# A two-layer block with gathered attention: the last group of tokens cut in two halves

## The chip, the cores and the metric

The kernel runs on one core of a Trainium2 chip. Its time is device time in microseconds (us), from the start of the program to its end; the median of 17 runs is 2808.39 us (2798.34 to 2819.59). A measurement of this kernel can tell about 0.2% from no change.

## The reference, cut to what matters

The input x holds 2048 tokens of 128 channels, float32. Two layers are applied, each an attention and a set of experts, each on a layernorm of x and added to x:

```
x = x + attention0(layernorm(x))   # 16 heads of 64, dense softmax over all 2048 tokens
x = x + experts0(layernorm(x))     # 16 gated experts, the best 4 of the best 2 of 4 groups, weighted
x = x + attention1(layernorm(x))   # 96 chosen tokens for each query, then softmax over these
x = x + experts1(layernorm(x))     # one shared gated expert and 2 of 8 experts by the token's number
```

For attention1 an indexer gives a score to every earlier token:

```
s_i = relu(einsum('bthd,bsd->bths', q_i, k_i));  I = einsum('bths,h->bts', s_i, idx_w)
I = where(local, inf, I); I = where(causal, -inf, I)      # the last 64 tokens are always chosen
_, idx = top_k(I, 96)
key, value = (c_kv @ W_uk)[idx], (c_kv @ W_uv)[idx]       # gathered for each query
```

So attention1 of a token needs experts0's result for that token and for all the tokens before it, since their keys may be chosen. experts0 and experts1 work on each token by itself.

## The kernel before

The 2048 tokens are 16 tiles of 128 tokens, and four tiles make a group: g = 0 to 3, tiles 4g to 4g+3. Attention 0 is a stream of units in `run` and takes most of the span. What follows it for a group is `follow(g)` (L588): `experts0`, `attention1`, `experts1`, in that order, each a generator whose yields carry a cost in us. For groups 0 to 2 it is advanced in small steps between the steps of attention 0 of the next group. For group 3 nothing is left beside it: `self.alone` is set, its PSUM tiles (`self.x`, L138) come from all eight banks in turn, and the generator is run through to its end. This stretch, from 2456 us on, is what the change touches; tiles 12 to 15 are its tokens.

What an engine does next is set by the order in which the program issues the work, with a scheduler that may move instructions on the engines' queues (not those marked to be kept in program order). SBUF pools are stacks on two sides, left and right; a new pool waits for the memory of what stood there before.

**First experts** (`experts0`, L599). For four tiles: the weights wb are loaded by SyncE (SP), six experts ahead; layernorm; four transposes on PE and a copy (`transposed`, L145); then `hidden` (L710) for the first four experts: the products p1 and p3 over 512 columns (L714, L715), Tanh and Identity on ACT (thb, zb; L718, L719), two instructions on DVE (hb; L721, L722). Then the gate: products pg, a sigmoid out of Exp, and the ranks by comparing all pairs (`below`), many small instructions on DVE; its weights are transposed on PE. Then expert after expert: `hidden` of expert e+4, the four products py of expert e-1 (one for each tile of 128 tokens) and four additions on DVE into the residual xr, which stays in SBUF.

**Second attention** (`attention1`, L727). It starts with a load of the ACT function set that holds Exp and Ln together. Preparation, for four tiles at once: layernorm, transposes, keys pk, softplus (L87 to L89: Exp, Ln on ACT, mu on DVE), a store of the keys kg into a table in HBM (SP), four products pm for the indexer's keys and queries, rotation of the keys and their transposes. Then, tile after tile:

- `index_scores(n)` (L792): the scores against all earlier tokens, in blocks of 512 columns by four heads: a product pi (L802), Relu on ACT into one of six buffers rl (L807), and an accumulation on DVE (L804, L808).
- `choose(n)` (L824): four rounds over all columns on DVE (the eight largest, their indices, and their removal: 11 passes), a transpose of the indices (ixT, L842), and then 32 indirect DMAs issued by POOL (`gather`, L853) that fetch the chosen tokens' keys from the table, 128 rows each.
- `queries(n)` (L866): loads of the local window by SP, the product pq, softplus on ACT, rotation on DVE, transposes ptq on PE into qT (three buffers).
- `attend(n)` (L913): rotation of the gathered keys kv, transposes ptr, products pl against the local window and the chosen keys (L956), maximum on DVE (mx, L962), Exp on ACT (L966), transposes, the products po, pj and at last xr += pj (L1013).

In the last group the order is written out: scores and choice of tiles 12 and 13; scores of 14 beside the queries of 12 and its choice beside the attention of 12; the same for 15 beside 13; then queries and attention of 14, then of 15.

**Last experts** (`experts1`, L1055), for four tiles at once: the ten weights wd are loaded, layernorm, transposes and a copy xT (L1069); two shared hidden layers (p1d, p3d); 16 small products ph for the eight experts, Gelu on ACT; the products pyd (L1097, L1102), yT (L1107), transposes pty (L1114), the sum o (L1116), and the store of the output.

Of the kernel before, what the change touches and what calls it, by code (L numbers as in the profile page):

```python
# [8 lines left out]
F32 = mybir.dt.float32  # L9
# [3 lines left out]
ALU = mybir.AluOpType  # L13
# [93 lines left out]
class Program:  # L107
# [37 lines left out]
    def transposed(self, src, dst, name):  # L145

        pt = self.x(name)
        for j in range(4):
            self.nc.tensor.transpose(pt[:, j, :], src[:, j, :], self.ident)
        self.nc.scalar.copy(dst, pt.rearrange("p a b -> p (a b)"))  # L150
# [437 lines left out]
    def follow(self, g):  # L588

        for stage in (self.experts0, self.attention1, self.experts1):  # L590
            with ExitStack() as sc:
                yield from stage(sc, g)
# [6 lines left out]
    def experts0(self, sc, g):  # L599
        nc, w, xr = self.nc, self.w, self.xr[g]  # L600
        sm = sc.enter_context(self.tc.tile_pool(name="b_sm", bufs=1, side="right"))

        ahead = 4 if self.alone else 0
        hp = sc.enter_context(self.tc.tile_pool(name="b_h", bufs=2 + ahead, side="right"))
        wp = sc.enter_context(self.tc.tile_pool(name="b_w", bufs=4 + ahead, side="right"))
        wx = [self.weights(wp, e, f"wb{g}_{e}") for e in range(2 + ahead)]
        xn = sm.tile([P, 4, C], F32, tag="xn", name=f"xn1_{g}")
        layernorm(nc, sm, xr, xn, "ln1")
        yield 5.0
        xT = sm.tile([P, 512], F32, tag="xT", name=f"xT1_{g}")  # L610
# [14 lines left out]
        pg = self.x(f"pg{g}", [P, 4, NE0])  # L625
        for j in range(4):
            nc.tensor.matmul(pg[:, j, :], xT[:, j * P : j * P + P], w["wg"], start=True, stop=True)
        s = sm.tile([P, 4, NE0], F32, tag="s", name=f"gs{g}")
# [8 lines left out]
        def below(v, n, first, k, tag):  # L637

            shape = [P, 4, n, n]
# [4 lines left out]
            ff = bcast(first.rearrange("p a b -> p (a b)"), 1, 4)  # L644
# [3 lines left out]
            rank = sm.tile([P, 4, n], F32, tag="rank" + tag, name=f"rank{tag}{g}")  # L648
# [4 lines left out]
        gm = sm.tile([P, 4, NG0], F32, tag="gm", name=f"gm{g}")  # L653
# [4 lines left out]
        goff = sm.tile([P, 4, NG0], F32, tag="goff", name=f"goff{g}")  # L658
        nc.vector.tensor_scalar(goff, gsel, 1.0, None, ALU.subtract)
        ms = sm.tile([P, 4, NE0], F32, tag="ms", name=f"ms{g}")  # L660
# [7 lines left out]
        we = sm.tile([P, 4, 32], F32, tag="we", name=f"we{g}")  # L668
        wh = sm.tile([P, 4, NE0], F32, tag="wh", name=f"wh{g}")
        nc.vector.memset(we, 0.0)  # L670
        nc.vector.tensor_tensor(we[:, :, 0:NE0], s, esel, ALU.mult)
        ws = sm.tile([P, 4], F32, tag="ws", name=f"ws{g}")
        wr = sm.tile([P, 4], F32, tag="wr", name=f"wr{g}")
# [6 lines left out]

        pt = self.x(f"ptw{g}", [P, P])
        nc.tensor.transpose(pt, we.rearrange("p a b -> p (a b)"), self.ident)
        wt = sm.tile([P, P], F32, tag="wt", name=f"wt{g}")
        nc.scalar.copy(wt, pt)
        yield 1.0
        pb = self.x(f"pb2_{g}")
        nc.tensor.matmul(pb.rearrange("p a b -> p (a b)"), wt, w["b2"], start=True, stop=True)
# [4 lines left out]
        for e in range(NE0 + 1):  # L692
# [5 lines left out]
            if e > 0:  # L698
                h = hs.pop(e - 1)
                py = self.x(f"py{g}_{e}")  # L700
                for j in range(4):
                    nc.tensor.matmul(py[:, j, :], h[:, j * P : j * P + P], wx[e - 1][:, 2, :], start=True, stop=True)
                yield 1.0
                for j in range(4):
# [5 lines left out]
    def hidden(self, pool, wx, xT, b1, hb1, b3, name):  # L710

        nc = self.nc
        p1, p3 = self.x("p1" + name, [P, 512]), self.x("p3" + name, [P, 512])
        nc.tensor.matmul(p1, wx[:, 0, :], xT, start=True, stop=True)  # L714
        nc.tensor.matmul(p3, wx[:, 1, :], xT, start=True, stop=True)  # L715
        th = pool.tile([P, 512], F32, tag="th", name="th" + name)
        z = pool.tile([P, 512], F32, tag="z", name="z" + name)
        nc.scalar.activation(th, p1, AF.Tanh, scale=0.5, bias=hb1)  # L718
        nc.scalar.activation(z, p1, AF.Identity, bias=b1)  # L719
        h = pool.tile([P, 512], F32, tag="h", name="h" + name)  # L720
# [4 lines left out]
    def attention1(self, sc, g):  # L725
# [7 lines left out]
        cols = slice(512 * g, 512 * g + 512)  # L733
# [4 lines left out]
        with ExitStack() as prep:  # L738
            pp = prep.enter_context(tc.tile_pool(name="c_prep", bufs=1, side="right"))
            xn = pp.tile([P, 4, C], F32, tag="xn", name=f"xn2_{g}")  # L740
            layernorm(nc, pp, xr, xn, "ln2")
            yield 5.0
            xT = pp.tile([P, 512], F32, tag="xT", name=f"xT2_{g}")
            self.transposed(xn, xT, f"pt2_{g}")
# [3 lines left out]
            pk = self.x(f"pk{g}", [P, 4, 64])  # L748
            for j in range(4):
                nc.tensor.matmul(pk[:, j, :], xT[:, j * P : j * P + P], w["wck"], start=True, stop=True)  # L750
            kg = pp.tile([P, 4, 64], F32, tag="kg", name=f"kg{g}")
# [494 lines left out]
```

## Time and profile before

| | |
|---|---|
| median of 17 runs | 2808.39 us (2798.34 to 2819.59) |
| the profiled execution | 2808.99 us |
| its span, first to last instruction | 2807.2 us |
| mean granted TensorE clock over the span | 0.938 |
| busy in the span: PE / DVE / ACT / POOL | 2543.4 (91%) / 1671.4 (60%) / 1789.5 (64%) / 674.1 us (24%) |
| the same up to 2456 us | 2320.0 / 1429.8 / 1659.7 / 544.0 us |
| the same from 2456 us on, 351.2 us | 223.5 / 241.6 / 129.8 / 130.1 us |

The busy shares of the whole span tell of attention 0, where PE works 94% of the time. In the last 351.2 us no engine is busy all the time: PE 64%, DVE 69%. A line of a timeline gives the start in us, the length in us, the engine, the line of the program, the operation, out<-in with the shapes, and in brackets the idle time of the engine before it and what ended it. "issue" there means that the engine waited for nothing that the profile shows. A line of the table of windows gives a stretch, its length, each engine's busy time with the number of its instructions, the granted TensorE clock, and what the DMA engines did.

### The profile page before, as it was taken

Reading aid. Unit: us, or ns where it says so; the run is one execution under the profiler, and the core shown is the slowest. Engines: PE = TensorE matmul, PEld = TensorE weight load, DVE = VectorE, ACT = ScalarE, POOL = GpSimd, SP = SyncE. Lnnn points to the kernel's source line nnn. Section 1 sums busy time; section 2 is a strip of 40 time slices with the busy share of each in tenths; the row PEclk is TensorE's granted clock in tenths of the full one; section 3 lists DMA queues with packets and bytes.
Section 4 is the critical chain, followed back from the end, with each engine's and each line's share of the span. In section 5 each row is a group of like instructions: output and inputs, shape, how many; then the busy total and the mean of one; then the engine's idle time right before and its main releaser. Section 6 shows DMA issues by size and latency. Waiting matters only on the chain. (4 is left out here: it accounts for less than half of the span.)

```text
span 2807.2 us, 39304 instructions
## 1 busy us (share of the span) xinstructions
PE 2543.4 (91%) x13452; PEld 1175.0 (42%) x13452; DVE 1671.4 (60%) x4650; ACT 1789.5 (64%) x4192; POOL 674.1 (24%) x964
## 2 busy tenths in 40 slices
PE   6999999999979999999999999999989999976566
PEld 3444444434434444434334444444433444442344
DVE  7655554566664454566686455466587754278863
ACT  3777778766656776856666677765656677533344
POOL 2111110000166620000065630000055460001771
PEclk9999999999999999999999999999999999986567
DMA  4322221111112211111111211111111120100111
GB/s 133 90 61 58 57 60 46 44 47 46 30 40 47 50 38 55 44 40 46 34 41 42 47 41 52 42 50 46 27 38 37 38 50 16 63 23 11 25 26 39
DMA packets 98103, 127.79 MB, mean 46 GB/s; under 512 B 31344, under 2 KB 49776, under 8 KB 97904
## 3 DMA queue, kind: packets, MB, share of 16 engines
q1 hardware_dynamic: 81520, 108.48, 13.8%
q0 software_dynamic: 16384, 16.81, 3.1%
q8 instruction: 106, 1.74, 0.3%
q14 instruction: 93, 0.76, 0.1%
HBM read 115.26 MB, written 9.96 MB: 45 GB/s over the span
## 5 line engine op out<-in xcount | busy, mean ns | idle before, releaser
L340 ACT ACTIVATE neg<-neg,mx 128x512 f32<-128x512 f32 x1024 | 729.8, 714 | 311.1 <-DVE neg L329 302.7
L329 DVE TENSOR_SCALAR_CACHE_REDUCE neg<-pa 128x512 f32<-128x512 f32 x1024 | 657.9, 685 | 430.1 <-PE pa L323 425.2
L390 ACT ACTIVATE e<-pb 128x512 f32<-128x512 f32 x1024 | 550.4, 595 | 296.5 <-PE pb L386 280.9
L384 PE MATMUL pb<-q,kb 64*128 64x512 f32 x2048 | 643.2, 631 | 7.4 <-DVE t_q L302 4.1
L323 PE MATMUL pa<-ka,q 64*128 64x512 f32 x2048 | 601.6, 623 | 19.3 <-ACT e L390 13.5
L853 POOL DMA_INDIRECT kv<-table,ixT x512 | 507.0, 990 | 425.7 <-DVE v L804 268.5
L399 PE MATMUL po<-e,ckv 128*64 128x512 f32 x2048 | 508.3, 610 | 0.0
L323 PEld LDWEIGHTS pa<-ka,q 64*128 64x128 f32 x2048 | 247.3, 191 | 225.7 <-issue 102.2
L303 POOL TENSOR_TENSOR q<-t_q 128x512 f32<-128x512 f32 x32 | 40.7, 1273 | 1200.8 <-DVE t_q L302 1099.8
L384 PEld LDWEIGHTS pb<-q,kb 64*128 64x128 f32 x2048 | 226.9, 190 | 209.0 <-issue 108.2
L386 PE MATMUL pb<-mrow,onesb 64*128 64x512 bf16 x1024 | 254.0, 385 | 8.1 <-ACT mrow L375 8.1
L399 PEld LDWEIGHTS po<-e,ckv 128*64 128x64 f32 x2048 | 126.7, 137 | 299.8 <-issue 282.3
L340 ACT ACTIVATION_READ_ACCUMULATOR neg<-neg,mx 128x1 f32 x1024 | 192.6, 188 | 0.0
L802 PE MATMUL pi<-kiT,qiT 64*128 64x512 f32 (+4 forms) x320 | 115.9, 624 | 24.8 <-DVE v L804 14.4
L850 POOL COPY at<-kv 128x1 f32<-128x1 f32 x378 | 80.0, 216 | 183.4 <-DMA kv<-table,ixT 176.8
L386 PEld LDWEIGHTS <-onesb 64*128 64x128 bf16 x1024 | 69.4, 96 | 128.6 <-issue 120.5
L418 DVE SCALAR_TENSOR_TENSOR xr<-pp,rs,xr 128x128 f32<-128x128 f32 x256 | 72.2, 344 | 84.5 <-PE pp L415 72.3
L721 DVE SCALAR_TENSOR_TENSOR hb<-thb,zb 128x512 f32<-128x512 f32 x64 | 44.3, 692 | 114.1 <-ACT zb L719 114.1
L808 DVE SCALAR_TENSOR_TENSOR v<-rl,iw_sb,v 128x512 f32<-128x512 f32 (+4 forms) x120 | 76.4, 642 | 50.7 <-ACT rl L807 46.6
L303 POOL TENSOR_TENSOR kst<-t_k 128x512 f32<-128x512 f32 x32 | 41.0, 1281 | 264.4 <-DVE t_k L302 168.5
L966 ACT ACTIVATE e<-pl,mx 128x208 f32<-128x208 f32 x128 | 54.3, 429 | 78.0 <-DVE mx L963 74.0
L962 DVE TENSOR_REDUCE mx<-pl 128x2 f32<-128x416 f32 x64 | 37.6, 590 | 97.2 <-PE pl L956 96.8
(276 smaller groups left out, 2862.9 us busy)
## 6 DMA issues: line engine op xcount, KB each, us to landing
ka<-kd SPq DMA_DIRECT2D x128, 256.0 KB
kb<-kd SPq DMA_DIRECT2D x128, 256.0 KB
wb<-in_wx SPq DMA_DIRECT2D x64, 192.0 KB
kd<-kst SPq DMA_DIRECT2D x32, 256.0 KB
kv<-table,ixT POOLq DMA_INDIRECT x512, 2.5
wd<-in_wx SPq DMA_DIRECT2D x40, 192.0 KB
csk<-in_cs SPq DMA_DIRECT2D x4, 512.0 KB
csq<-in_cs SPq DMA_DIRECT2D x4, 512.0 KB
```

Of the source, the lines that this page charges most:

```text
L303: nc.gpsimd.tensor_tensor(dst, t[:, 0, :], t[:, 1, :], ALU.add)
L323: nc.tensor.matmul(ps[h], q[rows, qt * P : qt * P + P], k[rows, :], start=True, stop=True)
L329: nc.vector.tensor_scalar(t, ps[h], -1.0, None, ALU.mult, ALU.min, accum_out=mx[at])
L340: nc.scalar.activation(t, t, AF.Exp, bias=mx[at], scale=-1.0, accum_out=su[at])
L384: nc.tensor.matmul(ps[h], k[rows, c], q[rows, :], start=True, stop=False)
L386: nc.tensor.matmul(ps[h], self.onesb[rows, :], mrow[rows, :], start=False, stop=True)
L390: nc.scalar.activation(e[:, h, :], ps[h], AF.Exp)
L399: nc.tensor.matmul(self.pos[u][cols, :], self.ckv[:, kb, :], e[:, h, :], start=(kb == 0), stop=(kb == NT - 1))
L802: nc.tensor.matmul(pi[:, : hi - lo], qiT[h // 2][rows, q], kiT[rows, lo:hi], start=True, stop=True)
L808: nc.vector.scalar_tensor_tensor(v[:, lo:hi], rl[:, : hi - lo], w["iw"][:, h : h + 1], v[:, lo:hi], ALU.mult, ALU.add)
L850: tc.keep_in_program_order(nc.gpsimd.tensor_copy(at[:, i : i + 1], slot))
L853: nc.gpsimd.indirect_dma_start(out=kv[:, 2 * (g % 16) + g // 16, :], out_offset=None, in_=table[0 : P * (n + 1), :], in_offset=bass.Indire ...
```

## The change

Only the last group is touched (`self.alone`); the functions take the first tile t0 and the number of tiles nt, and groups 0 to 2 call them with 0 and 4 as before.

- The first experts run for tiles 12 and 13, then the preparation for these two. The first experts of tiles 14 and 15 and their preparation (`rest`) are issued in between the scores and choices of tiles 12 and 13, two yields of `rest` for one of these. Products and ACT and DVE instructions that were 512 columns wide are 256 wide; the weights wb are loaded twice.
- The scores, choices, queries and attentions of 14 and 15 beside 12 and 13 keep their order.
- After the choice of 15: the weights wd are loaded; queries and attention of 14, queries of 15, then the last experts of tiles 12 and 13, the attention of 15, and the last experts of tiles 14 and 15. Each has its own store of the output.
- Alone, the pools of first and last experts stand on the left side; rl has four buffers instead of six, qT two instead of three.

In the built programs PE has 6323 instructions instead of 6227 (matrix products and transposes with their sequencer's rows), DVE 3247 instead of 3100, ACT 2968 instead of 2904, SP 472 instead of 454, POOL as many as before.

```
     def follow(self, g):
-        for stage in (self.experts0, self.attention1, self.experts1):
+        with ExitStack() as sc:
+            yield from self.experts0(sc, g, 0, 2 if self.alone else 4)
+        with ExitStack() as sc:
+            yield from self.attention1(sc, g)
+        if not self.alone:
             with ExitStack() as sc:
-                yield from stage(sc, g)
+                yield from self.experts1(sc, g, 0, 4, self.last_weights(sc, g))
...
-    def experts0(self, sc, g):
-        nc, w, xr = self.nc, self.w, self.xr[g]
+    def experts0(self, sc, g, t0, nt):
+        nc, w, xr = self.nc, self.w, self.xr[g][:, t0 : t0 + nt, :]
+        side, g = "left" if self.alone else "right", f"{g}_{t0}"
...
-                for j in range(4):
+                for j in range(nt):
                     nc.vector.scalar_tensor_tensor(
                         xr[:, j, :], py[:, j, :], wh[:, j, e - 1 : e], xr[:, j, :], ALU.mult, ALU.add
                     )
...
-        p1, p3 = self.x("p1" + name, [P, 512]), self.x("p3" + name, [P, 512])
+        n = xT.shape[1]
+        p1, p3 = self.x("p1" + name, [P, n]), self.x("p3" + name, [P, n])
...
-        with ExitStack() as prep:
+        def prepare(prep, t0, nt):
+            cols = slice(512 * g + P * t0, 512 * g + P * (t0 + nt))
+            part = slice(P * t0, P * (t0 + nt))
...
+        with ExitStack() as prep:
+            yield from prepare(prep, 0, 2 if self.alone else 4)
...
-                        rl = sm.tile([P, 512], F32, tag="rl", name=f"rl{n}_{lo}_{h}", bufs=6 if self.alone else 2)
+                        rl = sm.tile([P, 512], F32, tag="rl", name=f"rl{n}_{lo}_{h}", bufs=4 if self.alone else 2)
...
-                t = sm.tile([P, P, NH1], F32, tag=f"qT{i}", name=f"qT{n}_{i}", bufs=3 if self.alone else 1)
+                t = sm.tile([P, P, NH1], F32, tag=f"qT{i}", name=f"qT{n}_{i}", bufs=2 if self.alone else 1)
...
         if self.alone:
-            for m in range(n, n + 4):
-                if m < n + 2:
-                    yield from index_scores(m)
-                    yield from choose(m)
-                else:
-                    yield from beside(1, index_scores(m), queries(m - 2))
-                    yield from beside(3, choose(m), attend(m - 2))
-            for m in range(n + 2, n + 4):
-                yield from queries(m)
-                yield from attend(m)
+            def rest():
+                with ExitStack() as sb:
+                    yield from self.experts0(sb, g, 2, 2)
+                with ExitStack() as prep:
+                    yield from prepare(prep, 2, 2)
+
+            first = itertools.chain(*(f(m) for m in (n, n + 1) for f in (index_scores, choose)))
+            yield from beside(2, first, rest())
+            for m in (n + 2, n + 3):
+                yield from beside(1, index_scores(m), queries(m - 2))
+                yield from beside(3, choose(m), attend(m - 2))
+
+            with ExitStack() as sd:
+                wx = self.last_weights(sd, g)
+                yield from queries(n + 2)
+                yield from attend(n + 2)
+                yield from queries(n + 3)
+                with ExitStack() as sf:
+                    yield from self.experts1(sf, g, 0, 2, wx)
+                yield from attend(n + 3)
+                yield from self.experts1(sd, g, 2, 2, wx)
             return
...
-    def experts1(self, sc, g):
-        nc, w, xr = self.nc, self.w, self.xr[g]
-        sm = sc.enter_context(self.tc.tile_pool(name="d_sm", bufs=1, side="right"))
-        wp = sc.enter_context(self.tc.tile_pool(name="d_w", bufs=10, side="right"))
-        wx = [self.weights(wp, NE0 + i, f"wd{g}_{i}") for i in range(10)]
-        xn = sm.tile([P, 4, C], F32, tag="xn", name=f"xn3_{g}")
+    def experts1(self, sc, g, t0, nt, wx):
+        nc, w, xr = self.nc, self.w, self.xr[g][:, t0 : t0 + nt, :]
+        at, g, nj = 4 * g + t0, f"{g}_{t0}", 16 * nt
+        sm = sc.enter_context(self.tc.tile_pool(name="d_sm", bufs=1, side="left" if self.alone else "right"))
+        xn = sm.tile([P, nt, C], F32, tag="xn", name=f"xn3_{g}")
...
+    def last_weights(self, sc, g):
+        pool = sc.enter_context(self.tc.tile_pool(name="d_w", bufs=10, side="left" if self.alone else "right"))
+        return [self.weights(pool, NE0 + i, f"wd{g}_{i}") for i in range(10)]
```

## The prediction

> **What bounds the kernel now.** I read first the table of windows over the last 350 us of the span, cut at the borders of the last group's stages; then the timelines of POOL and DVE across those borders; then the chain that ended last. The two built programs show that nothing ahead of this stretch moves but a few short DVE instructions, so all of the answer lies here.
>
> ```profile
> core 0: us, PE busy (x) PEld busy (x) DVE busy (x) ACT busy (x) POOL busy (x), PEclk, DMA share, GB/s
> 2456.00:2527.00 71.00, 50.92 (x219) 31.05 (x216) 56.23 (x159) 22.52 (x36) 0.00 (x0) 0.83 0.08 23
> 2527.00:2543.00 16.00, 10.92 (x30) 5.47 (x32) 6.09 (x33) 4.66 (x10) 0.00 (x0) 0.58 0.05 9
> 2543.00:2582.00 39.00, 25.71 (x78) 9.43 (x74) 37.90 (x50) 14.88 (x32) 0.00 (x0) 0.68 0.06 8
> 2582.00:2711.00 129.00, 72.88 (x494) 42.54 (x494) 109.21 (x147) 43.69 (x107) 98.56 (x96) 0.57 0.14 25
> 2711.00:2753.00 42.00, 27.31 (x262) 21.83 (x262) 15.20 (x41) 23.62 (x61) 31.55 (x32) 0.70 0.14 26
> 2753.00:2777.00 24.00, 18.64 (x213) 14.33 (x212) 5.92 (x16) 13.04 (x37) 0.00 (x0) 0.71 0.01 3
> 2777.00:2807.00 30.00, 17.09 (x84) 11.51 (x84) 11.03 (x36) 7.37 (x9) 0.00 (x0) 0.73 0.23 75
> ```
>
> The rows are: first experts; preparation; scores and choice of tile 12; choices of 13 to 15 beside the gathers; the last gathers beside attention 14; attention 15; last experts. DVE is full in the third row and 85% busy in the fourth. The POOL and DVE timelines at their edges:
>
> ```profile
> 2582.76 1.52 POOL L853 DMA_INDIRECT kv<-table,ixT  x1 [257.00 <-DVE v L804]
> ...
> 2709.32 0.94 POOL L853 DMA_INDIRECT kv<-table,ixT  x1 [0.30 <-issue]
> 2711.97 0.94 POOL L853 DMA_INDIRECT kv<-table,ixT  x1 [1.71 <-issue]
> ...
> 2751.53 1.45 POOL L853 DMA_INDIRECT kv<-table,ixT  x1 [0.30 <-issue]
> ```
>
> ```profile
> 2711.02 0.21 DVE L842 STREAM_TRANSPOSE ixT<-ix 128x32 uint32<-128x32 uint32 x1
> 2716.10 0.29 DVE L1013 TENSOR_TENSOR xr<-xr,pj 128x128 f32<-128x128 f32 x1 [4.87 <-PE pj L1012]
> ...
> 2745.21 0.29 DVE L1013 TENSOR_TENSOR xr<-xr,pj 128x128 f32<-128x128 f32 x1 [10.80 <-PE pj L1012]
> ```
>
> Once started, the 128 gathers run almost without a gap, 42.2 us for 32; the one gap, 1.71 us, waits for tile 15's choice (call the end of the choice of tile n Tn: T12 2581.8, T13 2611.2, T14 2658.4, T15 2711.2). So POOL and DVE are balanced: DVE's list ends just when POOL runs dry. After T15 there is a second balance: attention 14 and the queries of 15 end on PE at 2753.1, the last gather at 2753.0. Only then come attention 15 (to 2776.9) and the last experts (to 2803.9, plus 3.3 for the output).
>
> **First experts by two tiles.** PE takes 2.61 us an expert in the steady part (p1 0.86, p3 0.86, py 0.89), DVE 2.31 (0.61+0.65 for hb, 4x0.26 for xr). DVE instructions shrink less than by half: 0.69 us at 128x512 (L721), 0.42 at 128x256 (mu, L89), so 0.34 and 0.38 start to start; two tiles cost 1.24 on DVE, 1.31 on PE. Gating: five 128x1024 instructions of 1.25 fall to about 0.7 (-2.7), small ones stay. Layernorm and transposes save 1.4, the first four experts about 4. The stage ends at 2500.6 instead of 2526.6: -26 (bounds -20, if ACT and semaphores hold an expert to 1.7 us, and -30). The weights now lie in memory that the big attention frees, behind its last loads on SP: issue 2453 to 2455 instead of 2404. At 0.49 us an issue and 0.6 us a load (192 KB at 323 GB/s in the last experts' loading) the first is there by 2458, needed at 2463.5; xn's layernorm covers it, without it up to 5 us.
>
> **Preparation by two tiles.** 16.5 us from the last xr to the first score becomes 11.8: the fixed chain of 14 tiny instructions (0.2 each) stays, four products at the half clock go from 1.7 to 0.86 each. The first score stands at 2512.4, 30.7 early.
>
> **Scores and choice of 12, now with the second half of the first experts between.** DVE order, counted: 11 passes over 1600 columns 19.6; scores 8.7; gating 7.5; 15 hidden layers 10.4; 18 additions to xr 4.7; rest 0.7: 51.6 us busy where before there were 37.9. Idle I add 8: Tanh's table load and the first four experts 5.5, the transposed gate weights 2.1 (3.3 in the row before). T12 = 2512.4 + 59.6 = 2572.0: 30.7 early has become 9.8.
>
> **T13.** 37.1 busy (choice 21.1, scores 9.2, the last 14 additions 3.6, layernorm and hidden rest) + 1.5 idle: 2610.6, level with before.
>
> **T14.** Before, 47.3 us, 5.4 of it a wait for gathers. Now tile 14's keys are prepared only here: 1.4 us of layernorm, then transposes, pk, four products, first score: 8.1 us, while DVE has nothing else in its order. Then 42.9 busy (scores 10.4, choice 22.8, queries and attention of 12 the rest) and 10 idle (6.0 as in tile 13's attention, where PE's pl is awaited; 2.5 for table loads, below; 1.5 at the first score): 61.0, T14 = 2671.6, 13.2 late. POOL has then been dry since 2657.
>
> **T15.** The same block as before (52.8) with one exposed table load: 54.1, T15 = 2725.7, **14.5 late**. As a check, DVE work from 2456.4 to T15 grows from 209 to 219 us, idle from 45 to 50.
>
> **Table loads.** The built order has 15 loads in this stretch instead of 3, because Tanh evicts the set that held both Exp and Ln; then Ln and Exp swap for every tile.
>
> ```profile
> 2783.34 1.02 ACT L1069 COPY xT<-pt 128x512 f32<-128x512 f32 x1 [10.28 <-issue]
> 2784.38 1.28 ACT L718 ACT_TABLE_LOAD   x1
> 2786.53 0.69 ACT L718 ACTIVATE thd<-p1d,hb 128x512 f32<-128x512 f32 x1 [0.87 <-PE p1d L714]
> ```
>
> A load takes 1.28 and waits for nothing, so it hides where ACT idles; Exp's loads ahead of the softmax do (ACT waits 2.0 there for tile 14), Ln's follow Exp directly and do not: 2.5 for tile 12 (two loads), 1.3 each for 13, 14, 15. [...] The rows show 1.28 (the instruction after 2419.27+1.28 starts at 2420.56).
>
> **After T15.** Before, 96.3: 5.1 to xr 13; 29.1 to xr 14; 7.9 queries 15; 23.9 attention 15; 27.0 layernorm and experts; 3.3 out. Now 5.1; 31.2 (one load, layernorm instructions between); 9.2 (one load); then the last experts of tiles 12 and 13, in PE's order between ptq and the transposes of kv 15, so wholly on the path; attention 15 at the pace of 14 (22.9); layernorm 4.1; experts again; out 3.2. One experts pass: 21.8 from its transposes to o, less 3.0 (p1, p3 by half), 0.9 (hb, Gelu), about 2.7 (copies, pyd, yT, pty, o); the 64 small products stay, 32 of them take 3.5 at 0.11 each whatever they stream: 15.0 and, second time, 14.7 (bounds 11.5 and 21.8, since no row has these at 32 columns). Sum 105.4: **9 longer**. The 42 us of tile 15's gathers would cover 42 us of work, but 60 stand there, and T14 to T15 leaves POOL so early that the gathers end at 2770, long before attention 15 at 2785.
>
> **Sum.** 2725.7 + 105.4 = 2831.1 of span, +23.9 on 2807.2. The profiled execution took 2808.99, 1.8 around its span and 0.6 above the median: 2832.
>
> **The other edits.** The fewer buffers (rl 6 to 4, qT 3 to 2) I cost at nothing: DVE, not ACT, paces the scores; if rl stalls, 0.5 us a block of four, 6 at most. SP: table<-kg of tiles 14 and 15 stands behind ten wd loads (4.9 us), but these wait only for the second experts, 10 us before kg; window loads follow it. The last output is half as large.
>
> **Rivals.** (a) The front's gain survives: PE and ACT fill DVE's waits better, first experts -30, the gap at 8.1 halved, T15 at 2714; end near 2820. For it: DVE idles 45 us before. Chance 0.19. (b) The interleaving stalls: 8 PSUM banks shared by p1, p3, py and pi, PE in order and at clock 0.5 as in the gathers' row; 1 us for each of 12 experts: 2844. Chance 0.15. (c) **Faster**: the gathers stay the bound. They begin at 2572.9 and need 168.8; the end is 2741.7 + 1.5 + 23.9 + 4.1 + 14.7 + 3.2 = 2789.1, 2791 with what lies around it. It decides if T15 falls by 2699 and the last experts fit beside the gathers; DVE's busy sum alone, 219 us from 2456.4, puts T15 at 2675 with no idle at all. Chance 0.10. (d) The halves cancel: T15 comes 9 us early and pays for the tail, 2809. Chance 0.07. That the order is not changed as said is excluded by the built order.
>
> **How the numbers follow.** Forecast 2832 (2824 to 2840), chance 0.49. The range 2815 to 2848 takes in (a) and most of (b); it leaves out (c), (d) and the upper part of (b), some 0.2. Faster by over 0.2% (5.6 us, about what a measurement of this kernel can tell from no change) is (c), 0.10; within it (d), 0.07; slower 0.83.
>
> **What would show it.** Right: ixT's four transposes at about 2572, 2611, 2672, 2726; POOL idle some 14 us ahead of tiles 14 and 15 each; 15 table loads; pyd of tiles 12 and 13 ahead of ptr of 15, and attention 15 starting well after its gathers. Wrong: gathers without a gap, or attention 15 waiting for kv.

## The result, and the profile after

The changed kernel takes 2867.14 us (median of 8 runs, 2861.54 to 2871.05) against 2807.4 us for the kernel before (46 runs): a ratio of 1.0209, 95% interval 1.0194 to 1.0223. It is slower by 59.7 us, where 24 were forecast and 2848 was the top of the range. The profiled execution has a span of 2865.7 us, 58.5 more than before.

The last addition of attention 0 into xr (xr<-pp) is the same event in all kernels; it moves by a few us from execution to execution, so all stages below are counted from it. Tn is again the end of tile n's choice, read here at the start of the transpose ixT, 0.2 us ahead of the forecast's reading; xr and o are read at the start of their additions.

| stage, us | before | forecast | after |
|---|---|---|---|
| attention 0 to T12 | 123.1 | 113.5 | 113.4 |
| to T13 | 29.3 | 38.6 | 43.8 |
| to T14 | 47.3 | 61.0 | 68.7 |
| to T15 | 52.8 | 54.1 | 56.9 |
| to xr of 13 | 5.1 | 5.1 | 5.1 |
| to xr of 14 | 29.1 | 31.2 | 32.7 |
| to o of tiles 12 and 13 | - | 24.2 | 30.5 |
| to xr of 15 | 31.7 | 22.9 | 27.2 |
| to the last o | 26.3 | 18.8 | 27.5 |
| to the end of the span | 4.0 | 3.2 | 3.7 |
| sum | 348.7 | 372.6 | 409.4 |

T12 and the first experts (to 2499.8, forecast 2500.6) came as worked out. From T12 to T15 the time is 15.7 longer than forecast, behind T15 21.2. The table of windows of the changed kernel, cut at these events (columns as before: busy us of PE, its weight loads, DVE, ACT, POOL, then the granted clock):

```profile
2500.00:2512.00 12.00, 7.68 (x22) 4.36 (x22) 6.30 (x50) 3.14 (x11) 0.00 (x0) 0.57 0.36 117
2512.00:2570.00 58.00, 42.02 (x153) 25.90 (x152) 51.63 (x110) 20.97 (x49) 0.00 (x0) 0.76 0.12 30
2570.00:2613.50 43.50, 17.93 (x48) 8.31 (x44) 37.53 (x68) 5.23 (x11) 31.28 (x32) 0.58 0.26 70
2613.50:2682.30 68.80, 46.25 (x271) 25.36 (x272) 46.80 (x77) 32.10 (x74) 31.22 (x32) 0.60 0.11 20
2682.30:2739.30 57.00, 36.59 (x257) 20.93 (x256) 45.03 (x65) 25.17 (x58) 32.96 (x32) 0.64 0.10 19
2739.30:2777.00 37.70, 25.93 (x245) 21.14 (x246) 13.70 (x47) 21.20 (x52) 28.14 (x30) 0.64 0.14 25
...
2786.00:2808.00 22.00, 18.24 (x94) 16.11 (x93) 3.79 (x9) 7.60 (x13) 0.00 (x0) 0.66 0.00 0
2808.00:2834.80 26.80, 20.99 (x211) 15.48 (x210) 7.20 (x20) 13.84 (x37) 0.00 (x0) 0.56 0.03 7
2834.80:2865.70 30.90, 20.72 (x80) 18.25 (x80) 7.22 (x27) 4.38 (x8) 0.00 (x0) 0.50 0.02 5
```

DVE's busy time to T15 is 220 us, as forecast (219). Its idle time is 63 us, 13 more than allowed: 6 in the third row (choice of 13), 22 in the fourth, 12 in the fifth. In the last three rows the granted clock falls from stage to stage and ends at 0.50 flat; 80 instructions of PE take 20.7 us there, 84 that stream twice the columns took 17.1 before. POOL, which had one gap of 1.71 us before, now waits twice:

```profile
2682.62 0.94 POOL L866 DMA_INDIRECT kv<-table,ixT  x1 [28.02 <-DVE ixT L855]
2740.02 0.94 POOL L866 DMA_INDIRECT kv<-table,ixT  x1 [14.99 <-issue]
...
2779.50 0.94 POOL L866 DMA_INDIRECT kv<-table,ixT  x1 [0.30 <-issue]
```

The gathers end at 2780.4, and attention 15 begins at 2807. So the gathers had long ceased to bind, as forecast.

### The profile page after: what moved, and what is told of

Read it like the earlier page. It is cut to its first block, busy times and chain, and to the rows that moved or that the text cites. A ratio compares the mean times of both kernels' runs of the same rounds, so it can differ in the third digit from the quotient of the medians.

```text
span 2865.7 us, 39838 instructions
## 1 busy us (share of the span) xinstructions
PE 2593.9 (91%) x13603; PEld 1221.5 (43%) x13603; DVE 1686.8 (59%) x4769; ACT 1814.3 (63%) x4256; POOL 670.3 (23%) x964
## 3 DMA queue, kind: packets, MB, share of 16 engines
q1 hardware_dynamic: 83856, 111.63, 13.9%
## 4 chain that ended last, share of the span: by engine, by line
PE 61%; DVE 14%; DMA 8%; ACT 7%; issue 4%; POOL 3%; SPq 0%; DVEq 0%; ACTq 0%; POOLq 0%
PE pb L385 13%; PE pa L324 12%; PE po L400 11%; DMA kv<-table,ixT 7%; DVE neg L330 3%; ACT neg L341 3%; POOL kv L866 3%; PE pb L387 3%; PE py L711 2%; PE p1b L724 2%; PE pp L416 2%; PE p3b L725 2%; PE pl L963 1%; PE pl L969 1%; DVE ix L850 1%
## 5 line engine op out<-in xcount | busy, mean ns | idle before, releaser
L866 POOL DMA_INDIRECT kv<-table,ixT x512 | 500.8, 978 | 460.0 <-DVE v L817 258.9
L400 PEld LDWEIGHTS po<-e,ckv 128*64 128x64 f32 x2048 | 126.8, 137 | 301.2 <-issue 284.7
L815 PE MATMUL pi<-kiT,qiT 64*128 64x512 f32 (+4 forms) x320 | 119.0, 624 | 16.2 <-DVE v L817 6.0
L731 DVE SCALAR_TENSOR_TENSOR hb<-thb,zb 128x512 f32<-128x512 f32 (+1 forms) x80 | 46.6, 583 | 113.7 <-ACT zb L729 113.6
L975 DVE TENSOR_REDUCE mx<-pl 128x2 f32<-128x416 f32 x64 | 37.7, 590 | 102.1 <-PE pl L969 101.7
```

What stands on the lines that cost most here:

```text
L400: nc.tensor.matmul(self.pos[u][cols, :], self.ckv[:, kb, :], e[:, h, :], start=(kb == 0), stop=(kb == NT - 1))
L815: nc.tensor.matmul(pi[:, : hi - lo], qiT[h // 2][rows, q], kiT[rows, lo:hi], start=True, stop=True)
L866: nc.gpsimd.indirect_dma_start(out=kv[:, 2 * (g % 16) + g // 16, :], out_offset=None, in_=table[0 : P * (n + 1), :], in_offset=bass.Indire ...
```

## The experiments

The front is what lies before T15, the end what lies behind it. Profiled stages in us, each from one profiled execution, and the ratio of the runs to the kernel before on the same chip. Where an edit leaves the front alone it still moved by up to 2.4 us (250.7 instead of 252.5, 280.4 instead of 282.8), so a difference of some 2 us in one profile says little.

| kernel | front | end | ratio (95% interval) |
|---|---|---|---|
| before | 252.5 | 96.2 | 1 |
| changed | 282.8 | 126.6 | 1.0209 (1.0194 to 1.0223) |
| last experts by four | 282.5 | 101.7 | 1.0127 (1.0095 to 1.0160) |
| first experts by four | 250.6 | 121.2 | 1.0074 (1.0053 to 1.0094) |
| keys of 14, 15 early | 266.6 | 126.8 | 1.0187 (1.0148 to 1.0226) |
| small products of 64 columns | 280.6 | 117.3 | 1.0170 (1.0133 to 1.0206) |
| one table load | 282.5 | 116.4 | 1.0171 (1.0138 to 1.0203) |
| rotation of 15 first | 280.4 | 123.3 | 1.0192 (1.0162 to 1.0222) |
| last experts beside attention 14 | 282.9 | 115.3 | 1.0170 (1.0134 to 1.0206) |
| early keys, one load, last by four | 272.2 | 102.0 | 1.0091 (1.0059 to 1.0123) |
| before, PE filled (18) | 250.7 | 93.0 | 1.0001 (0.9988 to 1.0015) |

Five more runs stand in two disturbed batches (told below), against the kernel before in the same batch: 64 columns with PE filled 1.0134 (1.0093 to 1.0174) and again 1.0181 (1.0134 to 1.0229), the first experts in two halves 1.0144 (1.0098 to 1.0189) and again 1.0126 (1.0072 to 1.0179), the kernel before with 12 filling products 1.0022 (0.9995 to 1.0049).

**Undoing one half of the change.** In the first kernel the last experts run once, for four tiles:

```
-    with ExitStack() as sf:
-        yield from self.experts1(sf, g, 0, 2, wx)
     yield from attend(n + 3)
-    yield from self.experts1(sd, g, 2, 2, wx)
+    yield from self.experts1(sd, g, 0, 4, wx)
```

> The changed kernel with its last experts again for four tiles at once, after attention 15; first experts by halves as changed. The profiled span after (2865.7 us) splits at the end of tile 15's choice: 2739.3 before it (2711.0 in the kernel before) and 126.4 behind it (96.3 before). Theory 1, the two halves of the loss are independent: the choice of 15 still ends near 2739, the rest takes the 96.3 of before plus up to 4 for ACT table loads, span 2836 to 2840, about 30 slower than before. Rival, the long end comes from elsewhere (colder PE, table loads, attention 14 and 15 themselves): the rest takes 110 or more, span above 2849.

In the second the first experts and the preparation do:

```
-    yield from self.experts0(sc, g, 0, 2 if self.alone else 4)
+    yield from self.experts0(sc, g, 0, 4)
...
-    yield from prepare(prep, 0, 2 if self.alone else 4)
+    yield from prepare(prep, 0, 4)
...
-    yield from beside(2, first, rest())
+    for m in (n, n + 1):
+        yield from index_scores(m)
+        yield from choose(m)
```

> The changed kernel with first experts and preparation again for four tiles at once, ahead of all scores; the last experts by halves as changed. Theory 1: the choice of 15 ends as in the kernel before, at 2711 to 2714 (fewer rl buffers may cost up to 3), and the end takes 120 to 126 (no exchange of ACT tables between Ln and Exp, up to 6 less than after): span 2831 to 2840. Rival, the long end is caused by the late front (a colder PE, gathers out of step): the end takes 105 or less, span below 2819.

Theory 1 holds, though both spans (2840.3 and 2830.2) lie just outside their ranges: 35.5 us remain with the split of the first experts alone, 23.0 with that of the last alone, together 58.5 of the 60.7. Within that the two losses add up. The second kernel keeps the fewer buffers of rl and qT, and its choices of 14 and 15 take 46.4 and 53.2 us (47.3 and 52.8 before): these buffers cost nothing that shows, as forecast. From xr of 15 to the last o, the last experts take 27.5 us for two tiles and 26.3 for four: halving them saved nothing, so one of the two passes is pure addition. (24.4 in two other kernels, told under the clock.)

**The clock.** 32 of the small products ph in the kernel before, and in the changed kernel PE in the small products of the first pass, then in the last pass:

```profile
2790.46 3.68 PE L1087 MATMUL ph<-xT,wd 128*128 128x64 f32 x32
```

```profile
2790.95 3.74 PE L1110 MATMUL ph<-xT,wd 128*128 128x32 f32 x32
...
2799.00 6.87 PE L1125 MATMUL pyd<-ge,wd 128*128 128x32 f32 x32
...
2842.84 1.06 PE L725 MATMUL p3d<-xT,wd 128*128 128x256 f32 x2
2843.70 6.88 PE L1110 MATMUL ph<-xT,wd 128*128 128x32 f32 x32
2850.38 1.20 PE L1120 MATMUL pyd<-hd,wd 128*128 128x256 f32 x2
2852.69 1.22 PE L1120 MATMUL pyd<-hd,wd 128*128 128x256 f32 x2 [1.11 <-DVE hd L732]
2853.70 6.87 PE L1125 MATMUL pyd<-ge,wd 128*128 128x32 f32 x32
```

In the first pass ph starts at the full clock and takes 0.11 us an instruction, as with 64 columns in the kernel before; but the granted clock falls to 0.50 at 2794.4, behind 3.4 us of these products, and pyd takes 0.21. In the last pass PE is never idle from 2840.1 to 2851.6, and yet the granted clock stays at 0.50: 0.21 us each. In the experiment each small product, and the two pyd products of the shared layers, stream their columns twice; the weights that they load, and what is kept of the result, stay the same:

```
-    ph = self.x(f"ph{g}_{k}", [P, 8, nj])
+    ph = self.x(f"ph{g}_{k}", [P, 8, wide, nj])
...
-    nc.tensor.matmul(ph[:, r, :], wx[2 + CHOSEN[r][k]][:, 0, :], xT[:, r, :], start=True, stop=True)
+    nc.tensor.matmul(ph[:, r, :, :], wx[2 + CHOSEN[r][k]][:, 0, :], bcast(xT[:, r, :], 1, wide), start=True, stop=True)
...
```

> The changed kernel, with every small product of its last experts (and their two pyd products of the shared layers) streaming its columns twice, so 64 instead of 32 columns (512 instead of 256), results as before. Theory 2: the granted clock stays or falls to 0.5 in the last experts because a product of 32 columns keeps PE occupied by its weights, not by its stream; with 64 columns 96 of the 128 small products that took 0.21 each take 0.11 again, span 2856 to 2860 (6 to 10 us shorter than after). Rival, only the pauses of PE between stages set the clock: nothing gets warmer, the wider products cost up to 3 us, span 2866 to 2869.

The timeline of PE there, in the last pass:

```profile
2834.80 1.06 PE L725 MATMUL p3d<-xT,wd 128*128 128x256 f32 x2
2835.65 4.46 PE L1111 MATMUL ph<-xT,wd 128*128 128x64 f32 x32
2839.95 1.08 PE L1125 MATMUL pyd<-hd,wd 128*128 128x512 f32 x2
...
2843.10 3.68 PE L1128 MATMUL pyd<-ge,wd 128*128 128x64 f32 x32
```

Twice the columns of ph in two thirds of the time (4.46 us instead of 6.88), and those of pyd in 3.68 instead of 6.87, which is what 32 products of 64 columns take at a granted 1.00 in the kernel before. From 2826.7 on the mean granted clock is 0.70, where it was 0.50. The pass takes 21.8 us instead of 27.5, and the end 117.3 instead of 126.6 (9.3 less, 6 to 10 expected). Part of the 5.7 in the pass can be chance: in two kernels with 32 columns (one table load, and last experts beside attention 14) the last pass took 24.4. The two ge, which wait for ph on DVE, start 2.10 and 1.95 us apart there instead of 3.41, and the mean granted clock of that stretch is 0.56 in the first of the two. But for pyd DVE waits 7.98 us there, as in the last pass of every profiled kernel with 32 columns; with 64 columns it waits 4.74. The pauses of PE in the pass are the same with 32 and 64 columns (4.31 and 4.32, 0.68, 1.11 and 0.71 us), and so are the weights loaded: in these runs the number of columns streamed makes the difference. The next one also fills PE's idle time ahead of the last experts and in the queries and attention of 15 with bf16 products whose results are overwritten:

```
+    for _ in range(k if self.alone else 0):
+        self.tc.keep_in_program_order(self.nc.tensor.matmul(out[:, 0:n], self.identb, rows, start=True, stop=True))
```

> The changed kernel with small products of 64 columns as in the run on them, and idle time of PE at the end filled by products whose result is overwritten: 18 (256 columns, bf16) ahead of the transposes of each of the two last experts, 10 and 8 (416 columns) ahead of the transposes ptq and pte of tile 15. Stretches are compared by what lies between xr of tile 14, o of the first half, xr of tile 15, o of the second half: 30.5, 27.2 and 27.5 us in the changed kernel, 28.2, 26.0 and 21.8 with 64 columns alone. Theory 2, the granted clock is what these stretches lack: o to xr 23 to 24, the last one 18 to 19.5, span 2846 to 2851 by the start of the changed kernel. Rival, the latencies of DVE and ACT between the products set these stretches: no stretch more than 1 us shorter than with 64 columns alone.

In two of the batches (this run, its repeat, both runs of two halves and the first filling of the kernel before) all kernels are slower, that before included (2922 us). The texts put on record call this late gathers; the traces don't bear that out. In the first filling of the kernel before POOL issues the gathers of a tile 1.25 us apart, as elsewhere, and DVE's longest wait for gathered keys in the last group is 2.47 us, against 5.38 in the kernel before. What is new is that DVE stands still while gathers are issued, for up to 37.3 us at a time, and that no instruction in the profile is named as what releases it; why is open. Ahead of the last group's first gather and behind its last no such standstill begins, so only stages there are read from these batches. The last pass of this run:

```profile
2940.93 3.63 PE L151 MATMUL pt<-smask_b,identb 128*128 128x256 bf16 x18
2945.27 0.58 PE L1105 MATMUL pt<-ident,xn 128*128 128x128 f32 x2 [0.70 <-DVE xn L78]
2946.53 0.70 PE L733 MATMUL p1d<-xT,wd 128*128 128x256 f32 x2 [0.68 <-ACT xT L1106]
2947.07 0.59 PE L734 MATMUL p3d<-xT,wd 128*128 128x256 f32 x2
...
2948.36 3.68 PE L1125 MATMUL ph<-xT,wd 128*128 128x64 f32 x32
```

Behind the filling p1d takes 0.70 us, p3d 0.59 and ph 3.68, as at a granted 1.00 in the first pass of the changed kernel (0.70, 0.59 and 3.74), and xr of 15 to o takes 18.9 us, as expected (18 to 19.5). That is the forecast's 18.8 for this stage. From its transposes to the end of o a pass takes 14.8 and 15.0 us in this run, where the changed kernel took 19.9 and 23.7. In the first pass the filling gained nothing all the same: from xr of 14 to the first o it is 29.0 us, 28.2 with 64 columns alone, since its 18 products stand on PE's path there for some 3 us. From the first o to xr of 15 it is 26.2, no better than with 64 columns alone (26.0), so the expectation of 23 to 24 there missed: its 16 transposes pte still took 3.41 us behind eight filling products of 2.96 us together (4.23 with 64 columns alone). The same kernel was run a second time:

> The changed kernel with small products of 64 columns and PE's idle time at the end filled, once more, for the same reason. Theory 2: choice of 15 to the end 107 to 114 us instead of 126.6 (117.3 with 64 columns alone), the last experts 18.5 to 19.5 from xr of 15 to o; median 1.014 to 1.016 of before. Rival: the filling delays other products, 117 or more.

The standstills came again, and the end (146.7) can't be read. The last pass took 20.5 us, over the 18.5 to 19.5 expected. The 1.6 us more than in the first run lie ahead of the first ge, which starts 3.25 us behind the last hd ahead of it, where it was 1.61; from there to o both runs take 9.6. The first stretch (28.9) and the second (26.2) came as in the first run. So the clock's price is shown for the last pass (8.6 or 7.0 of 27.5 us) and, by 64 columns, in part for the first (30.5 to 28.2, near what a stage moves by itself); for the rest of the end it stays open.

**Tile 14's keys.** DVE's timeline in the changed kernel, between the scores and the end of tile 13's choice. The small lines are the layernorm of tiles 14 and 15, one link of its chain between two passes over 1728 columns:

```profile
2591.04 1.96 DVE L848 MAX8 m<-v 128x8 f32<-128x1728 f32 x1
2592.92 0.15 DVE L75 TENSOR_SCALAR ln2v<-ln2mv 128x2 f32<-128x2 f32 x1
...
2597.03 0.16 DVE L58 TENSOR_SCALAR ln2r<-ln2g 128x2 uint32<-128x2 uint32 x1
...
2599.03 0.14 DVE L60 TENSOR_TENSOR ln2w<-ln2r 128x2 f32<-128x2 f32 x1
...
2613.44 0.21 DVE L855 STREAM_TRANSPOSE ixT<-ix 128x32 uint32<-128x32 uint32 x1
...
2614.35 0.63 DVE L78 TENSOR_SCALAR xn<-xr,ln2mv,ln2r 128x128 f32<-128x128 f32 x2
```

A chain of 3 us takes 24. The experiment pins the first pass of the choice behind it (the pinning itself is not printed here):

```
+    first = itertools.chain(index_scores(n), choose(n), index_scores(n + 1))
+    yield from beside(2, first, half())
...
+    rest = prepare(prep, 2, 2)
+    yield next(rest)
+    yield from beside(2, choose(n + 1, True), rest)
```

> The changed kernel with the layernorm ahead of the keys of tiles 14 and 15 kept in one piece in front of tile 13's choice (in the changed kernel its 14 tiny DVE instructions stand one by one between the choice's 11 passes, so the keys are ready 24 us later); the rest of this preparation runs beside that choice. Theory 4, tile 14 is late because its scores cannot start before those keys: choice 13 ends some 3 us later (2616), choice 14 no later than 50 us behind it (68.7 in the changed kernel, 47.3 in the kernel before), 2660 to 2666, choice 15 at 2714 to 2721, span 2841 to 2848. Rival, the scores and attentions themselves are slow there (colder PE, table loads, four rl buffers): choice 14 stays 60 us or more behind choice 13, span above 2857.

Choice 13 takes 46.2 us instead of 43.8, choice 14 52.9 instead of 68.7, and the front gets 16.2 shorter: theory 4 by the stages, though 2.9 over its 50, and the span (2854.7) missed its 2841 to 2848, 5.0 of it because attention 0 ended that much later in this execution. The medians alone (1.0187) would not have told it: 16.2 us would make 1.0151, at the lower edge of the interval. But a second kernel with the same edit, the one with early keys, one load and last experts by four below, has 52.5 for choice 14 too.

**The ACT tables.** The pattern that the forecast priced is in the timeline of ACT, between the queries of 12 and the scores of 14:

```profile
2624.53 0.63 ACT L820 ACTIVATE rl<-pi 128x512 f32<-128x512 f32 x1
2625.18 1.28 ACT L87 ACT_TABLE_LOAD   x1
2626.47 0.42 ACT L87 ACTIVATE spqa<-spqa 128x256 f32<-128x256 f32 x1
2626.79 0.58 ACT L820 ACTIVATE rl<-pi 128x512 f32<-128x512 f32 x1
2627.39 1.28 ACT L88 ACT_TABLE_LOAD   x1
```

The experiment adds one line behind the first experts of 14 and 15. In the traces 30 loads remain of 38, 8 fewer and not the 12 that were expected:

```
+    tc.keep_in_program_order(nc.scalar.preload_act_table_set("natural_log_exp_and_others"))
```

> The changed kernel with one more load of the ACT function set that holds both Exp and Ln, behind the first experts of tiles 14 and 15, so that 13 loads of single functions between there and the last attention go (12 fewer in the built order). Theory 3, as the prediction priced it: five exposed loads of 1.28 are on the path, span 2858 to 2861 (5 to 8 us shorter). Rival, they are all in time in which ACT would have waited: span within 1.5 us of 2865.7. Second rival: each load costs more than its 1.28 us because the engine behind ACT waits too, span below 2855.

In the profile 10.5 us are gone, between theory 3 and its second rival. 3.1 of them lie in the last pass, where no load was removed: it is one of the two with 24.4 us, in which ph was faster. The other 7.4 lie about where the forecast put them, if they are counted up to the ends of the attentions: 3.3 less to T14 (2.5 forecast for tile 12), then 1.3 less to xr of 13, 1.9 to xr of 14, 1.1 to the first o (1.3 forecast for each). T15 hides this: the choice of 15 ends 2.5 later behind T14, but xr of 13 comes only 1.2 behind it instead of 5.1. In the rows above a load takes 1.28 us, starts 0.02 us behind the instruction ahead of it, and the instruction behind the first load starts 0.01 us after its end: a load costs ACT 1.28 us there, with 0.03 around it. The loads of Exp ahead of the softmax, which the forecast let hide, start 0.08 us behind the end of mx on DVE for tiles 12, 13 and 14, after ACT had idled 5.15, 4.81 and 0.58 us: these three did not hide.

**The order at the end.** The rotation of tile 15's gathered keys is pinned on DVE and stood behind the first pass' o, though its gathers had ended 27 us earlier (at 2780.4):

```profile
2807.31 0.42 DVE L1139 TENSOR_TENSOR o<-xr,pty 128x256 f32<-128x256 f32 x1 [0.78 <-PE pty L1137]
2807.68 0.69 DVE L97 TENSOR_TENSOR w<-kv,cs 128x512 f32<-128x512 f32 x1
```

One experiment issues it first, the other runs the first pass beside attention 14:

```
+    last = attend(n + 3)
+    yield next(last) + next(last)
     with ExitStack() as sf:
         yield from self.experts1(sf, g, 0, 2, wx)
```

> The changed kernel with the rotation of the gathered keys of tile 15 (DVE) issued in front of the last experts of tiles 12 and 13 instead of behind them; nothing else moves by hand. Theory 5: attention 15 lost 3 to 4 us because this rotation, pinned in program order, stood behind those experts' sum o although its gathers had ended 27 us earlier: span 2860 to 2863. Rival: PE is the one that is late there (half clock), the rotation was hidden: less than 1.5 us, span 2864 to 2867.

```
...
+    yield from beside(1, attend(n + 2), self.experts1(sf, g, 0, 2, wx))
+    yield from queries(n + 3)
+    yield from attend(n + 3)
```

> The changed kernel with the last experts of tiles 12 and 13 issued step by step beside attention 14, while the gathers of tile 15 run, instead of between the queries and the attention of 15. Theory 1: 19.9 us of the end path go, attention 14 gets 6 to 10 longer since PE works 26 of 38 us there already; span 2852 to 2859. Rival, PE in its order makes attention 14 wait for each step of the experts (table loads too): the two together take as long as one behind the other, span above 2862.

Rotation first: from the first o to xr of 15 22.6 us instead of 27.2, from xr of 14 to that o 31.8 instead of 30.5; the end 3.3 shorter, as theory 5 has it. Part of it is PE's pace: four products pl of 80 columns take 0.67 us there, 1.14 in the changed kernel, where the granted clock is 0.50. Beside attention 14: xr of 13 to xr of 14 takes 46.9 instead of 32.7 us, the end 115.3, that is 11.3 less. 3.1 of these lie in the last pass, which this edit leaves alone (ph was faster there, as in the run with one table load); the other 8.2 are some two fifths of the pass, hidden. The end is still 19 us more than that of the kernel before.

**What is left of the front.** Early keys, one table load and last experts by four tiles together:

> First experts by halves as changed, with the early layernorm of the run on it, one load of the joint table set behind them, and the last experts for four tiles at once as in the kernel before. Theory: what is left of the loss is DVE's longer list (some 10 us more to the choice of 15, less the time in which it idled): choice of 15 at 2712 to 2718, end 96 to 98 behind it, span 2808 to 2816, that is 0 to 9 slower than before. Rival, the choice of 12 being 12 us earlier is worth its time once the stalls are gone: the gathers decide, span 2795 to 2804, faster than before.

The front is 272.2, 19.7 over before; the theory's 2808 to 2816 missed (2826.1), the rival too, and the end of 102.0 missed its 96 to 98. Early keys alone had left less of the loss (266.6, 14.1 over before): with one load added the choice of 13 takes 50.6 us instead of 46.2, DVE idling 7 us in it instead of 3; why was not followed up. To see whether halving alone costs this, the two halves were put one behind the other ahead of everything, all else as before:

```
+    for t0 in (0, 2) if self.alone else (0,):
+        with ExitStack() as sc:
+            yield from self.experts0(sc, g, t0, 2 if self.alone else 4)
```

> The kernel before in its order, but for the first experts: tiles 12 and 13, then tiles 14 and 15, one half behind the other, both ahead of the preparation of all four; last experts for four tiles at once. It prices the halving of the first experts without any interleaving with scores. From the rows: a half took 43.5 us (end of attention 0 to its last xr) against 68.0 for all four, so up to 87 for two, less what the second half's first products overlap. Theory, halving by itself costs what the front lost: choice of 12 comes 12 to 19 later than in the kernel before, all the rest equal, span 2819 to 2828. Rival, the scheduler runs the two halves into one another: under 8 later, span below 2816, and the loss of the front is the interleaving's alone.

> The first experts in two halves, one behind the other, without interleaving, once more, since the gathers of that batch landed late in every kernel, the kernel before included. What is open is whether halving alone makes up the front's loss of 30.3 us (end of attention 0 to the choice of 15: 252.5 before, 282.8 changed, 272.2 with early keys and one table load). Theory: choice of 12 some 15 us later than in the kernel before and the stages behind it as there (29.3, 47, 53), so 266 to 270 to the choice of 15, median 1.004 to 1.007 of before. Rival: the later stages get longer too, over 272, so something else than the halves' own length is lost.

T12 came 138.8 and 140.3 us behind attention 0, 123.1 before: halving costs 15.7 to 17.2 us by itself, with T13 29.3 behind T12 in both, as before. That agrees with the rows: 43.5 us for two tiles, 68.0 for four. The choices of 14 and 15 lie among the standstills and can't be read in these batches; nor do the medians (1.0144 and 1.0126, where 1.004 to 1.007 was expected) price the halving. So halving by itself costs as much as the 14.1 that early keys leave, and all but some 4 us of the 19.7; that the interleaving adds nothing of its own is not shown.

**Filling PE in the kernel before.** If the clock is worth so much, the kernel before should gain too:

> The kernel before, with the same filling of PE's idle time (12 products ahead of the last experts' transposes, 10 ahead of ptq and 8 ahead of pte of tile 15, 416 columns, results overwritten). Theory 2: xr of tile 15 comes 30 us behind xr of 14 instead of 31.7, o 22.5 to 23.5 behind it instead of 26.3, together 4 to 6 us, 2802 to 2805 in the median, faster than before by 0.15 to 0.2%. Rival: the products delay the work behind them as much as the clock gives, within 1.5 us.

> The kernel before with PE's idle time at the end filled more fully: 18 products of 416 columns (bf16, overwritten) ahead of the last experts' transposes instead of 12, 16 and 12 ahead of ptq and pte of tile 15. With 12 the filling ended 1.8 us ahead of the transposes and the clock rose only 9.5 us after them. Theory 2: the first shared products (p1d, p3d) run at the full clock, xr of tile 15 to o takes 22.5 to 23.5 us instead of 26.3, xr of 14 to xr of 15 takes 28 to 29 instead of 31.7, median 0.1 to 0.25% under the kernel before. Rival: 18 products of 0.35 delay the transposes by a microsecond and the clock rises no earlier; the stretch stays at 26 to 27.5, no change in the median.

With 12 products the last pass took 26.3 us as without:

```profile
2883.10 3.48 PE L151 MATMUL pt<-smask_b,identb 128*128 128x416 bf16 x12
2888.38 1.15 PE L1082 MATMUL pt<-ident,xn 128*128 128x128 f32 x4 [1.80 <-DVE xn L78]
2890.69 2.08 PE L723 MATMUL p1d<-xT,wd 128*128 128x512 f32 x2 [1.15 <-ACT xT L1083]
```

The expectation for 18 says that the clock rose only 9.5 us behind this filling. Read from the rows, p1d takes 2.08 us, as in the kernel before at a granted 0.50, and the last p3d, from 2895.9 on, 1.02. But the twelve filling products took 0.29 us each, while eight took 1.58 us (0.20 each) behind pl of 0.35 in the same run and 2.96 (0.37 each) behind pl of 0.53 in the run with 64 columns and filling. By this estimate the clock had risen within the filling, and was lost by the first p1d, behind PE's pauses of 1.80 and 1.15 us, not late. With 18:

```profile
2778.03 4.65 PE L151 MATMUL pt<-smask_b,identb 128*128 128x416 bf16 x18
2783.33 1.00 PE L1082 MATMUL pt<-ident,xn 128*128 128x128 f32 x4 [0.65 <-DVE xn L78]
2785.49 1.12 PE L723 MATMUL p1d<-xT,wd 128*128 128x512 f32 x2 [1.15 <-ACT xT L1083]
```

The first pause is 0.65 us, and the first products p1d take 1.12 us instead of 2.08; the pass takes 24.0 instead of 26.3 (22.5 to 23.5 expected). From xr of 14 to xr of 15 it is 31.2, where 28 to 29 was expected (28.7 with 8 products ahead of pte, whose 12 now take 3.5 us on the path). The end is 3.2 us shorter in the profile, but the median does not move (1.0001; the interval reaches down to 0.9988, 3.4 us), so no version was found that beats the kernel before.

## Why the prediction was wrong

- **Right: the mechanism and the side.** DVE's longer list delays the choices, the gathers run dry ahead of 14 and 15, and two passes of the last experts stand on the path where one stood. DVE's work (219 against 220 us), T12 (113.5 against 113.4), the first experts, the 15 table loads and the order of PE came as worked out. The two fewer buffers cost nothing.
- **Wrong, the largest: the term "the last experts" behind T15**, 15.0 and 14.7 with "32 of them take 3.5 at 0.11 each whatever they stream". That row was read at the full clock, for 64 columns; "whatever they stream" no row of the kernel before shows, and with 32 columns 32 of them took 3.74 us at the full clock, 6.88 at a granted 0.50. From its transposes to o a pass measured 19.9 and 23.7, the second outside the bounds of 11.5 and 21.8 too, because at 32 columns the granted clock fell to 0.50 (first pass) or stayed there (last pass) and a small product took 0.21. 13.9 of the 21.2 us lie here. With 64 columns and PE filled, 32 small products taking 3.68, a pass took 14.8 and 15.0. That this meets the forecast is in part luck: of those passes p1d and p3d are 1.8 us, where the forecast left 3.0 of the 6.0 before, so its other terms were some 1.2 short. (Its own subtractions give 15.2, not 15.0.) The step carried the duration of a row over to a shape at which the clock was not that of the row.
- **Wrong in size: attention 15 "at the pace of 14 (22.9)"** took 27.2: a granted clock of 0.56 in that row, and its rotation of keys behind the experts' o in DVE's order, a wait that the forecast had not seen. Issued first, the stage took 22.6.
- **Wrong in size: T13 and T14.** For T13 1.5 us of idle were allowed and 6 came, DVE waiting for py and rl while the clock was 0.58. For T14 the late keys were seen (8.1 us to the first score, 8.2 measured), but the scores behind them got only 4 us of idle time, and 9.7 came: PE and ACT, which ran ahead of DVE in the kernel before, are followed step by step. What the late keys took is 15.8 us in the run without them, of which 2.4 came back in the choice of 13.
- **Right in size and, nearly, in place: table loads**, 6.4 forecast, 7.4 measured without the clock's share.
- **The rivals**: interleaving stalls (b) were named with the clock, at 1 us for each of 12 experts up to T12. T12 had none of it; the price came one stage later, and nothing in the forecast carried the clock behind T15.

What moves the clock was not shown beyond this. In the first pass of the changed kernel it rose at 2787.6 and fell at 2794.4; in the last pass PE was occupied for 11.5 us on end (2840.1 to 2851.6) at 0.50.

## What to carry to other kernels

Halving a stage halves only what scales with its width: here two halves of the first experts took 16 us more than the whole, and half of the last experts as long as all of them (27.5 us against 26.3), until wider products and filling brought them to 18.9. Before a row's duration is carried to a narrower shape, ask at which granted clock it was taken, and measure whether the narrower products keep it: here 32 products of 32 columns took 6.88 us in the last pass, where 32 of 64 columns had taken 3.68. And when a short chain is put beside long instructions on the same engine, look in the built order for whether each of its links waits for one of them: 3 us became 24.

## What the runs showed of the hardware

In the last pass of the changed kernel 32-column float32 products with a 128x128 weight load each stayed at a granted 0.50 for 6.9 us twice (0.21 us each), though PE was occupied throughout; in the first pass the clock fell from 1.00 to 0.50 behind 3.4 us of them. The same products with 64 columns took 4.46 us for the first 32 and 3.68 for the next 32 (0.11 each, as at a granted 1.00 in the kernel before). Streaming every column twice made the end 9.3 us shorter, of which up to 3.1 can be chance. Behind 3.48 us of filling and a pause of PE of 1.80 us p1d took 2.08 us; behind 4.65 us and a pause of 0.65 us it took 1.12. And in two batches on two chips DVE stood still for up to 37.3 us at a time while gathers were issued, and the kernel before took 2922 and 2920 us instead of 2807; one of these chips gave 2811 in another batch.
